# A first layernorm transposed on VectorE, a router on four column parts of the array, and scatters that keep their place

## The chip, the cores and the metric

The kernel runs on one core of a Trainium2 chip. A core has engines with streams of instructions of their own: TensorE (PE in the profile; PEld is its loading of weights), VectorE (DVE), ScalarE (ACT), GpSimd (POOL) and SyncE (SP, which here only issues transfers). They wait for one another by semaphores. Operands lie in SBUF, an on-chip memory of 128 partitions; TensorE writes to PSUM, which the other engines read. Transfers to and from the chip's main memory (DRAM) are queued by an engine and carried out by DMA engines.

The metric is the time of one execution in microseconds (us), the median of several runs. Everything is computed in 32-bit floats.

## The reference

Four batches (B) of 512 tokens (L) with 512 features (D) go through a cross-attention without softmax, against a context of 1024 rows (S), and then through a mixture of eight experts (E), two for each token. There are 16 heads of 32 features (HD).

```python
def attention(query, kv, Wq, Wg, bg, Wkv, Wo):
    q = query @ Wq.T
    gate = sigmoid(query @ Wg.T + bg)
    k, v = split(kv @ Wkv.T, 2, axis=-1)
    q, k = feature_map(q), feature_map(k)     # where(x > 0, x + 1, exp(x)), head by head
    kv_summary = einsum("bhsd,bhse->bhde", k, v)
    z = 1.0 / (einsum("bhld,bhd->bhl", q, k.sum(axis=-2))[..., None] + EPS)
    attn = einsum("bhld,bhde->bhle", q, kv_summary) * z
    return attn * gate @ Wo.T

def experts(x, Wr, We, be):
    w, sel = top_k(einsum("bsd,de->bse", x, Wr), 2)
    w = softmax(w)
    # sum over the two chosen experts e of w_e * (x @ We[e] + be[e])

x = x + attention(layernorm(x), context, ...)
x = x + experts(layernorm(x), Wr, We, be)
```

A layernorm subtracts the mean of a token's 512 features and multiplies by the reciprocal of their standard deviation. There is one ahead of the attention (the first) and one ahead of the router and the experts (the second).

## The kernel before

A matmul on TensorE sums over partitions, so what is summed over must lie there. Tokens come from DRAM in rows (a tile is 128 tokens, one in each partition, by 512 features); for the products with wq, wg and the router the features must be in the partitions, and so a tile has to be turned.

**Keys and values** (`kv_tiles`). A batch's context has eight tiles of 128 rows, brought in turned already (cT). For each, `keys` has four matmuls to pk and `feature_map` (line 221: ex on DVE, 222: its exponential on ACT, 223: k on DVE); `values` has four to pv and a copy on ACT; `kv_add` sums k and v of the tile before into kvs, with four matmuls. One such turn holds TensorE for 7.8 us.

**First layernorm** (`layernorm_stats`, `normalized_T`). Lines 229 to 233 make mean and variance (mv) and rstd for four tiles of x. Each tile is then normalised on DVE (line 237, to xn), turned by four 128x128 transposes on TensorE through PSUM (line 94, to pt) and copied by ACT to xT (line 246). In the first batch this is done in the turns of tiles 3 to 6; for later batches in turns 4 to 7, after the attention's output of the batch before (`between` in the main loop).

**Query, gate, output.** `query` and `gate` have four groups of four matmuls each (pq, pg). `inverses` computes the denominators (pd) with four matmuls that use 32 of the array's columns each, beside one another (`tile_position`). `products` makes the rest, and `attention_out` multiplies by wo and adds to x on DVE (line 434).

**Router** (`choose`, a generator that yields between its steps). The second layernorm writes four tiles row, each of 512 features and two numbers more; they are turned as above (to x2T), and four matmuls a tile, of 128 tokens' features against eight columns of wr, give the logits pl. In batches 0 to 2 one tile's step stands in each of the turns 4 to 7 of the next batch's keys; in the last batch the steps stand among expert tiles. The top two are found on DVE by small operations (lines 499 to 513).

**Dispatch** (`dispatch`) computes on TensorE (pp, from both and acc, lines 524 to 530) the place of each token in the list of its expert, and POOL scatters the rows to stream in DRAM by eight indirect transfers (line 563). For batch b this stands inside the queries of batch b + 1.

**Experts** (`run`). A tile of 128 tokens of one expert is read from stream (xg, in four pieces of 32 partitions, and of, which holds two numbers for each token; line 704), turned on DVE by a block transpose (line 721: each 32x32 block is turned in place, and the loads and weights are laid out so that this suffices), multiplied (pe), the bias added on DVE (y, line 753), and scattered to result in DRAM by POOL (line 757). 17 tiles are run before the last dispatch's rows are there, and 18 more after; a branch behind them (`tc.If(many > SURE)`) holds tiles that this data does not need.

**The end.** `fetch` reads the two results of each token back (line 827), `add` weighs and adds them to x (line 840), `store` writes out (line 851). The list `begins` says after which expert tile each of 14 tiles of tokens is fetched; the last two are fetched after the branch by SP and ACT.

**What sets the order.** Matmuls and transposes stay in the order of the program, as do SP's loads (`load`, line 100). On POOL, `mark` puts a tiny memset ahead of a transfer, so that it keeps its place. The others are placed by a scheduler, tied at points by `issue_after`. A tile's buffer can be written again when all that used its contents are done; the pool big has one buffer for each tag (xT, aT), tag row has four, one for each tile. SP's transfers share eight semaphores in turn, so that a transfer also waits for the one eight places ahead of it.

Of the kernel before, what the change touches and what calls it, by code (L numbers as in the profile page):

```python
# [9 lines left out]
F32 = mybir.dt.float32  # L10
# [3 lines left out]
ALU = mybir.AluOpType  # L14
# [3 lines left out]
P = 128  # L18
B, L, S, D = 4, 512, 1024, 512
E, F = 8, 512  # L20
HD = 32
NC = D // P
NT = L // P
# [30 lines left out]
def xattn_moe_kernel(  # L54
# [32 lines left out]
    result = dram.tile([NOWHERE + 2 * L, F], F32, name="result")  # L87


    def matmul(**operands):  # L90
        tc.keep_in_program_order(nc.tensor.matmul(**operands))  # L91

# [6 lines left out]
    def load(dst, src):  # L99
        latest["load"] = nc.sync.dma_start(out=dst, in_=src)  # L100
        tc.keep_in_program_order(latest["load"])

    def load_ctx(b, s):
# [2 lines left out]
        load(t, cT[b, s])  # L106
        return t

    def load_x(b):
        tiles = []  # L110
        for t in range(NT):
            xt = xpool.tile([P, D], F32, tag="x", name=f"x_{b}_{t}")
            load(xt, x[b, t])
            tiles.append(xt)
        return tiles

    wkv_sb = wpool.tile([P, NC, 2 * D], F32, tag="wkv", name="wkv_sb")
    wq_sb = wpool.tile([P, NC, D], F32, tag="wq", name="wq_sb")
    wg_sb = wpool.tile([P, NC, D], F32, tag="wg", name="wg_sb")
    wo_sb = wpool.tile([P, NC, D], F32, tag="wo", name="wo_sb")  # L120
    wr_sb = wpool.tile([P, NC, E], F32, name="wr_sb")
    bg_sb = wpool.tile([P, NC], F32, name="bg_sb")


    we_sb = wpool.tile([P, E, NC, F], F32, name="we_sb")
    we_rows = we.rearrange("e (c f) i n -> e i f c n", f=HD)

# [16 lines left out]
    turned = [(g, 0, g * HD, P - g * HD) for g in range(NC)]  # L144
    turned += [(g, P - g * HD, 0, g * HD) for g in range(1, NC)]
    wg_in = big.tile([P, NC, D], F32, tag="aT", name="wg_in")
    load(wg_in, wg)
    for g, a, b, n in turned:
        nc.gpsimd.tensor_copy(
            wg_sb[:, :, g * P + b : g * P + b + n], wg_in[:, :, g * P + a : g * P + a + n]  # L150
        )
        load(bg_sb[b : b + n, g : g + 1], bg[a : a + n, g : g + 1])
    load(wq_sb, wq)
    load(wr_sb, wr)
    for g, a, b, n in turned:
        load(wo_sb[b : b + n, g, :], wo[a : a + n, g, :])


    ident = const.tile([P, P], F32, name="ident")
# [18 lines left out]
    for g in range(NC):  # L178
        r = slice(g * HD, (g + 1) * HD)
        for i in range(NC):  # L180
            o = (i + g) % NC
            nc.gpsimd.affine_select(
                out=spread[r, o, :], in_=spread[r, o, :], pattern=[[0, HD]],
                compare_op=ALU.is_equal, fill=0.0, base=-i, channel_multiplier=1,
            )

    ones = const.tile([P, P], F32, name="ones")
    nc.gpsimd.memset(ones, 1.0)
# [29 lines left out]
    def feature_map(dst, src):  # L218

        ex = work.tile([P, D], F32, tag="ex", name="ex")  # L220
        nc.vector.tensor_scalar(ex, src, 0.0, None, ALU.min)  # L221
        nc.scalar.activation(ex, ex, AF.Exp)  # L222
        nc.vector.scalar_tensor_tensor(dst, src, 0.0, ex, ALU.max, ALU.add)  # L223

    def layernorm_stats(tiles):
        mv = small.tile([P, NT, 2], F32, tag="mv", name="mv")
        for t in range(NT):
            st = small.tile([P, 6], F32, tag="st", name="st")
            nc.vector.bn_stats(st, tiles[t])
            nc.vector.bn_aggr(mv[:, t, :], st)  # L230
        rstd = small.tile([P, NT], F32, tag="rstd", name="rstd")
        nc.scalar.activation(rstd, mv[:, :, 1], AF.Sqrt, bias=eps_sb)
        nc.vector.reciprocal(rstd, rstd)
        return mv, rstd

    def normalize(dst, xt, t, mv, rstd):
        nc.vector.tensor_scalar(
            dst, xt, mv[:, t, 0:1], rstd[:, t : t + 1], ALU.subtract, ALU.mult
        )

    def transposed(dst, src):

        pt = pmm.tile([P, NC, P], F32, tag="mm", name="pt")
        for c in range(NC):
            transpose(pt[:, c, :], src[:, ts(c, P)])
        nc.scalar.copy(dst, pt)

    def normalized_T(xT, t, tiles, mv, rstd):

        xn = work.tile([P, D], F32, tag="ex", name="xn")  # L250
        normalize(xn, tiles[t], t, mv, rstd)
        transposed(xT[:, :, ts(t, P)], xn)

    def new_xT():
        return big.tile([P, NC, L], F32, tag="xT", name="xT")
# [199 lines left out]
    def mark():  # L455

        tc.keep_in_program_order(nc.gpsimd.memset(marked, 0.0))
# [12 lines left out]

    def choose(b, mv, rstd):

        pl = pmm.tile([P, NT, E], F32, tag="mm", name="pl")
        rows, xTs = [], []
        for t in range(NT):
            row = work.tile([P, ROW], F32, tag="row", name="row", bufs=NT)
            normalize(row[:, 0:D], xs[b][t], t, mv, rstd)
            nc.gpsimd.tensor_copy(row[:, D : D + 1], home[:, b * NT + t : b * NT + t + 1])
            rows.append(row)

        def logits(t):
            for c in range(NC):
                matmul(
                    out=pl[:, t, :],
                    lhsT=xTs[t][:, c, :],
                    rhs=wr_sb[:, c, :],
                    start=(c == 0),
                    stop=(c == NC - 1),
                )

        for t in range(NT):
            xTs.append(work.tile([P, NC, P], F32, tag="z", name="x2T"))
            transposed(xTs[t], rows[t])
            if t > 0:
                logits(t - 1)
            yield
        logits(NT - 1)
        lg = small.tile([P, NT, E], F32, tag="lg", name="lg")
        nc.vector.tensor_copy(lg, pl)

        def largest(name):
            m = small.tile([P, NT, 1], F32, tag=f"m{name}", name=f"m{name}")
            hot = small.tile([P, NT, E], F32, tag=f"hot{name}", name=f"hot{name}")
            at = small.tile([P, NT, 1], F32, tag=f"at{name}", name=f"at{name}")
            nc.vector.tensor_reduce(m, lg, AX.X, ALU.max)
            nc.vector.tensor_tensor(hot, lg, m.to_broadcast([P, NT, E]), ALU.is_equal)
            nc.vector.tensor_tensor(hot, hot, rank, ALU.mult)
            nc.vector.tensor_reduce(at, hot, AX.X, ALU.max)
            nc.vector.tensor_tensor(hot, hot, at.to_broadcast([P, NT, E]), ALU.is_equal)
            return m, hot, at  # L510

        m1, hot1, first = largest("1")
        nc.vector.scalar_tensor_tensor(lg, hot1, -BIG, lg, ALU.mult, ALU.add)
        m2, hot2, _ = largest("2")

        routed[b] = rows, m1, hot1, first, m2, hot2
        yield
# [292 lines left out]
    def fetch(t, tiles, queue, group=None):  # L810

        pool, tag = homes[t // 2 % len(homes)]
        if t not in fetched:
            pair = pool.tile([P, 2, 2, F], F32, tag=tag, name=f"y_{t}")
            fetched[t], fetched[t + 1] = pair[:, 0], pair[:, 1]
        if group is None:
            src = flat[:, t]
        else:
            if group not in rows_of:
                rows_of[group] = nc.values_load(  # L820
                    spots[0:1, group : group + 1], [queue.engine], min_val=0, max_val=NOWHERE,
                    skip_runtime_bounds_check_because="one of two constants",
                )
            row = rows_of[group] + (t - READ[group][0]) * 2 * P
            src = result[ds(row, 2 * P), :].rearrange("(p i) f -> p i f", i=2)
        mark()
        load = queue.dma_start(out=fetched[t], in_=src)
        behind(load, written["result"][:tiles], "results of the tokens")
        for put in written["result"][tiles:]:
            tc.declare_no_dep(load.ins, put.ins, reason=read_again)  # L830
        tc.keep_in_program_order(load)
        read_back.append(load)
# [31 lines left out]
    def plan(step, *what):  # L864
        at_step.setdefault(min(step, SURE), []).append(what)

    begins = (-3, -2, -1, 0, 5, 6, 7, 8, 10, 11, 14, 15, SURE - 1, SURE - 1)
    for g, (lo, hi, most) in enumerate(READ):
        for t in range(lo, hi):
            plan(begins[t], fetch, t, most, nc.gpsimd, g)  # L870
# [9 lines left out]

    xT = new_xT()
    kv_tiles(0, 0, 3)
    ln = layernorm_stats(xs[0])
    kv_tiles(0, 3, NS, lambda i: i < NT and normalized_T(xT, i, xs[0], *ln))
    kv_blocks(sums[0])
    for b in range(B):
        more = b + 1 < B
# [42 lines left out]
        next(product)  # L930
        if more:
            xs[b + 1] = load_x(b + 1)
            kv_tiles(b + 1, 0, NS // 2, inside=lambda: next(product))
        else:
            next(early)
            next(product)
            for _ in range(3):
                next(early)
        attention_out(b, aT)
        choice = choose(b, *layernorm_stats(xs[b]))  # L940
        if more:
            ln = layernorm_stats(xs[b + 1])
            xT = new_xT()

            def between(i):
                normalized_T(xT, i, xs[b + 1], *ln)
                next(choice)

            kv_tiles(b + 1, NS // 2, NS, between)
            next(choice)  # L950
            kv_blocks(sums[b + 1])
    for _ in range(2):
# [3 lines left out]
        if t % 2:  # L956
            next(early)
    next(choice)
    for _ in range(2):
        next(early)  # L960
    dispatch(B - 1)
    for _ in range(2):
        next(early)
# [113 lines left out]
```

## Time and profile before

| | |
|---|---|
| median of 3 runs | 621.65 us (619.83 to 622.51) |
| profiled execution | 622.61 us, span 621.0 us |
| mean granted TensorE clock | 0.983 |
| PE busy | 588.5 us, 95% of the span, 1908 instructions |
| DVE busy | 271.0 us, 44%, 668 instructions |
| ACT busy | 115.2 us, 19%, 180 instructions |
| POOL busy | 100.6 us, 16%, 274 instructions |
| DMA | 105.55 MB, mean 170 GB/s |

The span runs from the first instruction to the last. The slices divide it into 40 equal stretches, and each digit is the busy share of one in tenths. In a group of instructions by line, the columns are line, engine, operation, output<-inputs with shapes and how often; busy time and the mean duration in ns; and the engine's idle time just ahead of them with what ended it. A line of the timeline has a start in us, a duration in us (of the first to the last of the group that follow one another), engine, line and operation. A line of the chain has a start, the time that this step adds to the chain, the engine or DMA and what it did; a q behind an engine's name is its sequencer, which also issues transfers.

### The profile page before, as it was taken

What the parts mean: (1) busy time and instruction counts of PE and PEld (TensorE: products, weight loads), DVE (VectorE), ACT (ScalarE), POOL (GpSimd) and SP (SyncE); (2) the same over time, 40 slices, a digit from 0 to 9 for tenths busy, and PEclk for the clock granted to TensorE, in tenths of its full rate; (3) what the DMA queues carried; (4) which work ended last, traced back from release to release, by engine and by line L of the source; (5) the groups of instructions that cost most, each with busy time, mean ns of one, the idle gap of its engine ahead of it and who ended that gap; (6) DMA issues with size and microseconds to landing.
All of it is one profiled execution on the core that took longest, in us unless ns stands there. A gap on an engine that the chain in (4) does not pass through costs nothing. (4 is left out here: it accounts for less than half of the span.)

```text
span 621.0 us, 6578 instructions
## 1 busy us (share of the span) xinstructions
PE 588.5 (95%) x1908; PEld 286.3 (46%) x1908; DVE 271.0 (44%) x668; ACT 115.2 (19%) x180; POOL 100.6 (16%) x274
## 2 busy tenths in 40 slices
PE   7999999999999999999999999999999999999940
PEld 3555543454565335446643454565434554443410
DVE  2222243216215341351454226127874569475663
ACT  1322222112322221142222211322210100000000
POOL 4100000000002200000050000002311227455540
PEclk9999999999999999999999999999999999999985
DMA  8648920682686227527530660933344444889965
GB/s 317 191 158 301 293 81 2 167 240 69 164 248 184 81 86 237 153 85 221 186 137 1 203 204 0 327 130 137 116 114 119 96 119 177 262 243 259 296 219 173
DMA packets 68597, 105.55 MB, mean 170 GB/s; under 512 B 11981, under 2 KB 30413, under 8 KB 68176
## 3 DMA queue, kind: packets, MB, share of 16 engines
q1 hardware_dynamic: 58944, 76.24, 41.7%
q0 software_dynamic: 8176, 26.78, 12.1%
q10 hardware_dynamic: 1440, 2.10, 1.1%
q8 instruction: 16, 0.26, 0.2%
q14 instruction: 21, 0.17, 0.1%
HBM read 45.93 MB, written 59.94 MB: 170 GB/s over the span
## 5 line engine op out<-in xcount | busy, mean ns | idle before, releaser
L91 PE MATMUL pk<-wkv_sb,cT 128*128 128x512 f32 x256 | 118.6, 607 | 4.4 <-DMA cT<-in_cT_dram 4.4
L91 PE MATMUL pv<-wkv_sb,cT 128*128 128x512 f32 x256 | 115.2, 593 | 0.0
L221 DVE TENSOR_SCALAR ex<-pk 128x512 f32<-128x512 f32 x32 | 22.0, 688 | 148.3 <-PE pk L91 148.3
L91 PEld LDWEIGHTS pv<-wkv_sb,cT 128*128 128x128 f32 x256 | 48.4, 190 | 62.3 <-issue 59.3
L91 PEld LDWEIGHTS pk<-wkv_sb,cT 128*128 128x128 f32 x256 | 47.7, 194 | 57.8 <-issue 49.9
L91 PE MATMUL pe<-we_sb,xgT 128*128 x144 | 62.8, 595 | 0.6 <-DVE xgT L721 0.6
L91 PE MATMUL pe<-we_sb,turned_rows 128*128 x136 | 60.3, 597 | 0.7 <-DVE turned_rows L721 0.7
L278 POOL MEMSET v<- 128x4 f32 x32 | 3.3, 105 | 345.3 <-PE kvs L91 282.3
L91 PE MATMUL pg<-xT,wg_sb 128*128 128x512 f32 x128 | 56.7, 596 | 0.0
L91 PE MATMUL pq<-xT,wq_sb 128*128 128x512 f32 x128 | 56.6, 596 | 0.0
L91 PE MATMUL po<-wo_sb,aT 128*128 128x512 f32 x128 | 55.6, 592 | 0.0
L222 ACT ACTIVATE ex<-ex 128x512 f32<-128x512 f32 x48 | 30.2, 630 | 136.2 <-DVE ex L221 126.6
L757 POOL DMA_INDIRECT result<-y,to x35 | 35.8, 1023 | 93.7 <-DVE y L753 88.4
L91 PEld LDWEIGHTS pe<-we_sb,xgT 128*128 128x128 f32 x144 | 27.0, 190 | 36.3 <-issue 29.9
L91 PEld LDWEIGHTS pe<-we_sb,turned_rows 128*128 128x128 f32 x136 | 25.3, 190 | 32.4 <-issue 29.5
L563 POOL DMA_INDIRECT stream<-row,slot x32 | 31.9, 996 | 50.3 <-DVE cmp L591 22.5
L91 PEld LDWEIGHTS kvs<-v,k 128*128 128x128 f32 x256 | 33.3, 191 | 13.4 <-issue 13.4
L91 PEld LDWEIGHTS pg<-xT,wg_sb 128*128 128x128 f32 x128 | 24.0, 190 | 32.1 <-issue 32.1
L91 PEld LDWEIGHTS po<-wo_sb,aT 128*128 128x128 f32 x128 | 24.1, 190 | 29.2 <-issue 28.7
L91 PEld LDWEIGHTS pq<-xT,wq_sb 128*128 128x128 f32 x128 | 23.8, 190 | 27.3 <-issue 27.3
L91 PE MATMUL kvs<-v,k 128*128 128x129 f32 x256 | 34.0, 275 | 0.0
L223 DVE SCALAR_TENSOR_TENSOR k<-pk,ex 128x512 f32<-128x512 f32 x32 | 22.1, 690 | 19.5 <-ACT ex L222 19.5
(175 smaller groups left out, 465.1 us busy)
## 6 DMA issues: line engine op xcount, KB each, us to landing
stream<-empty SPq DMA_DIRECT2D x24, 1028.0 KB, 8.1
stream<-empty SPq DMA_DIRECT2D x8, 1285.0 KB, 6.8
xg<-stream SPq DMA_DIRECT2D x140, 64.0 KB, 2.7
we_sb<-in_we_dram SPq DMA_DIRECT2D x32, 256.0 KB, 5.5
cT<-in_cT_dram SPq DMA_DIRECT2D x31, 256.0 KB, 3.1
y<-result POOLq DMA_DIRECT2D x14, 512.0 KB, 5.5
x<-in_x_dram SPq DMA_DIRECT2D x16, 256.0 KB, 6.6
out_dram<-y POOLq DMA_DIRECT2D x10, 256.0 KB, 4.6
```

Source lines behind the costliest of these rows:

```text
L91: tc.keep_in_program_order(nc.tensor.matmul(**operands))
L221: nc.vector.tensor_scalar(ex, src, 0.0, None, ALU.min)
L222: nc.scalar.activation(ex, ex, AF.Exp)
L223: nc.vector.scalar_tensor_tensor(dst, src, 0.0, ex, ALU.max, ALU.add)
L278: nc.gpsimd.memset(v[:, :, P : P + 1], 1.0)
L563: put = nc.gpsimd.indirect_dma_start(out=stream, out_offset=bass.IndirectOffsetOnAxis(ap=slots[i][:, t, :], axis=0), in_=rows[t], in_offse ...
L757: put = nc.gpsimd.indirect_dma_start(out=result, out_offset=bass.IndirectOffsetOnAxis(ap=home_i, axis=0), in_=y, in_offset=None, bounds_ch ...
```

## The change

**First layernorm.** x is brought in a second time, as blocks (`load_blocks`): partition 32 i + t holds chunk i (128 features) of the tokens t, 32 + t and so on, in runs of 512 bytes. For blocks, mean and rstd must lie otherwise than `layernorm_stats` leaves them: `spread_moments` writes them from POOL to moments in DRAM and reads them back into ln. `normalized_T` then has four operations of 128x128 on DVE for a tile, and one block transpose of 128x512 straight to xT. In xT the features have another order within the partitions; wq and wg are loaded in the same order (`load_rows`). Both are placed in turns 0 to 3 of the next batch's keys, ahead of the attention's output, no longer in turns 4 to 7. The first batch's stay in turns 3 to 6.

**Router.** All four tiles of row are turned first, to one x2T of 512 tokens. Four matmuls, one for each chunk of 128 features, against wr padded with zeros to 32 columns, stand on four column parts and write four shares of the logits to ps. ACT copies ps to share, and four matmuls with the constant by_expert add the shares and turn the result: pl. `choose` yields once more. The four tiles of row are one tile now, whose buffer the blocks also use (tag row, one buffer).

**Order.** wo is loaded after the first three turns, not before. `fetch` has a mark ahead of its values_load, and the last pair of fetches in `begins` stands one expert tile earlier. In the last batch, one expert tile instead of two stands between the router's last matmuls and dispatch, one more between ps and pl.

```diff
+    moments = dram.tile([B, HD, NT, P // HD, 2], F32, name="moments")
...
+    def load_blocks(b):
+        blocks = work.tile([P, NT, ROW], F32, tag="row", name="blocks", bufs=1)
+        blocks = blocks.rearrange("p t r -> p (t r)")[:, 0 : NT * D]
+        for i in range(NC):
+            load(
+                blocks[ts(i, HD), :].rearrange("t (n f) -> t n f", f=P),
+                x[b, :, :, ts(i, P)].rearrange("k (j t) f -> t (k j) f", t=HD),
+            )
+        return blocks
...
+    def load_rows(dst, w):
+        for i in range(NC):
+            load(dst[ts(i, HD)], w.rearrange("(c f) i n -> i f c n", f=HD)[i])
...
-    wr_sb = wpool.tile([P, NC, E], F32, name="wr_sb")
+    wr_sb = wpool.tile([P, NC, HD], F32, name="wr_sb")
+    nc.gpsimd.memset(wr_sb, 0.0)
...
-    load(wg_in, wg)
+    load_rows(wg_in, wg)
...
-    load(wq_sb, wq)
-    load(wr_sb, wr)
-    for g, a, b, n in turned:
-        load(wo_sb[b : b + n, g, :], wo[a : a + n, g, :])
+    load_rows(wq_sb, wq)
+    blocks = load_blocks(0)
+    load(wr_sb[:, :, 0:E], wr)
...
+    by_expert = const.tile([P, E], F32, name="by_expert")
+    nc.gpsimd.memset(by_expert, 1.0)
+    for c in range(NC):
+        nc.gpsimd.affine_select(
+            out=by_expert[ts(c, HD), :], in_=by_expert[ts(c, HD), :], pattern=[[1, E]],
+            compare_op=ALU.is_equal, fill=0.0, base=0, channel_multiplier=-1,
+        )
...
-        nc.vector.scalar_tensor_tensor(dst, src, 0.0, ex, ALU.max, ALU.add)
+        latest["map"] = nc.vector.scalar_tensor_tensor(dst, src, 0.0, ex, ALU.max, ALU.add)
...
-    def normalized_T(xT, t, tiles, mv, rstd):
-
-        xn = work.tile([P, D], F32, tag="ex", name="xn")
-        normalize(xn, tiles[t], t, mv, rstd)
-        transposed(xT[:, :, ts(t, P)], xn)
+    def spread_moments(b, tiles):
+
+        mv, rstd = layernorm_stats(tiles)
+        for k, of in enumerate((mv[:, :, 0], rstd)):
+            nc.gpsimd.dma_start(
+                out=moments[b, :, :, :, k].rearrange("t n j -> j t n"), in_=of
+            )
+        ln = small.tile([P, NT, P // HD, 2], F32, tag="ln", name="ln", bufs=1)
+        for i in range(NC):
+            nc.gpsimd.dma_start(
+                out=ln[ts(i, HD)].rearrange("t n j k -> t (n j k)"),
+                in_=moments[b].rearrange("t n j k -> t (n j k)"),
+            )
+        return ln
+
+    def normalized_T(xT, t, blocks, ln):
+
+        rows = blocks[:, ts(t, D)].rearrange("p (j f) -> p j f", f=P)
+        with tc.issue_after(latest["map"].ins):
+            for j in range(P // HD):
+                nc.vector.tensor_scalar(
+                    rows[:, j], rows[:, j], ln[:, t, j, 0:1], ln[:, t, j, 1:2],
+                    ALU.subtract, ALU.mult,
+                )
+            nc.vector.transpose(
+                xT[:, :, ts(t, P)].rearrange("p c (j t) -> p j c t", t=HD),
+                rows.rearrange("p j (c f) -> p j c f", f=HD),
+            )
...
+        batch = work.tile([P, NT, ROW], F32, tag="row", name="rows", bufs=1)
...
-        def logits(t):
-            for c in range(NC):
-                matmul(
-                    out=pl[:, t, :],
-                    lhsT=xTs[t][:, c, :],
-                    rhs=wr_sb[:, c, :],
-                    start=(c == 0),
-                    stop=(c == NC - 1),
-                )
...
-            xTs.append(work.tile([P, NC, P], F32, tag="z", name="x2T"))
-            transposed(xTs[t], rows[t])
-            if t > 0:
-                logits(t - 1)
+            transposed(xT[:, :, ts(t, P)], rows[t])
             yield
-        logits(NT - 1)
+
+        ps = pmm.tile([P, L], F32, tag="mm", name="ps")
+        for c in range(NC):
+            matmul(
+                out=ps[ts(c, HD), :],
+                lhsT=wr_sb[:, c, :],
+                rhs=xT[:, c, :],
+                start=True,
+                stop=True,
+                tile_position=(0, c * HD),
+            )
+        share = work.tile([P, L], F32, tag="z", name="share")
+        nc.scalar.copy(share, ps)
+        yield
+        pl = pmm.tile([P, NT, E], F32, tag="mm", name="pl")
+        for t in range(NT):
+            matmul(
+                out=pl[:, t, :], lhsT=share[:, ts(t, P)], rhs=by_expert, start=True, stop=True
+            )
...
             if group not in rows_of:
+                mark()
...
-    begins = (-3, -2, -1, 0, 5, 6, 7, 8, 10, 11, 14, 15, SURE - 1, SURE - 1)
+    begins = (-3, -2, -1, 0, 5, 6, 7, 8, 10, 11, 14, 15, SURE - 2, SURE - 2)
...
     kv_tiles(0, 0, 3)
-    ln = layernorm_stats(xs[0])
-    kv_tiles(0, 3, NS, lambda i: i < NT and normalized_T(xT, i, xs[0], *ln))
+    for g, a, b, n in turned:
+        load(wo_sb[b : b + n, g, :], wo[a : a + n, g, :])
+    ln = spread_moments(0, xs[0])
+    kv_tiles(0, 3, NS, lambda i: i < NT and normalized_T(xT, i, blocks, ln))
...
-            kv_tiles(b + 1, 0, NS // 2, inside=lambda: next(product))
+            blocks = load_blocks(b + 1)
+            xT = new_xT()
+
+            def between(i):
+                if i == 0:
+                    ln.append(spread_moments(b + 1, xs[b + 1]))
+                else:
+                    for t in {1: (0,), 2: (1,), 3: (2, 3)}[i]:
+                        normalized_T(xT, t, blocks, ln[0])
+
+            ln = []
+            kv_tiles(b + 1, 0, NS // 2, between, inside=lambda: next(product))
...
-            ln = layernorm_stats(xs[b + 1])
-            xT = new_xT()
-
-            def between(i):
-                normalized_T(xT, i, xs[b + 1], *ln)
-                next(choice)
-
-            kv_tiles(b + 1, NS // 2, NS, between)
+            kv_tiles(b + 1, NS // 2, NS, lambda i: next(choice))
+            next(choice)
             next(choice)
             kv_blocks(sums[b + 1])
...
     next(choice)
-    for _ in range(2):
-        next(early)
+    next(early)
+    next(choice)
+    next(early)
     dispatch(B - 1)
```

More of the change, by code (lines that the diff above doesn't have):

```diff
@@ L471, in choose @@
     def choose(b, mv, rstd):
-        pl = pmm.tile([P, NT, E], F32, tag="mm", name="pl")
-        rows, xTs = [], []
+        rows = []
+        batch = work.tile([P, NT, ROW], F32, tag="row", name="rows", bufs=1)
         for t in range(NT):
-            row = work.tile([P, ROW], F32, tag="row", name="row", bufs=NT)
+            row = batch[:, t, :]
             normalize(row[:, 0:D], xs[b][t], t, mv, rstd)
@@ L479, in choose @@
             rows.append(row)
-        def logits(t):
-            for c in range(NC):
-                matmul(
-                    out=pl[:, t, :],
-                    lhsT=xTs[t][:, c, :],
-                    rhs=wr_sb[:, c, :],
-                    start=(c == 0),
-                    stop=(c == NC - 1),
-                )
+        xT = big.tile([P, NC, L], F32, tag="aT", name="x2T")
         for t in range(NT):
-            xTs.append(work.tile([P, NC, P], F32, tag="z", name="x2T"))
-            transposed(xTs[t], rows[t])
-            if t > 0:
-                logits(t - 1)
+            transposed(xT[:, :, ts(t, P)], rows[t])
             yield
-        logits(NT - 1)
+        ps = pmm.tile([P, L], F32, tag="mm", name="ps")
[16 more added lines that the diff above has]
+            )
         lg = small.tile([P, NT, E], F32, tag="lg", name="lg")
```

## The prediction

> **What bounds the kernel now.** I read the page's busy times first, then its slices, the groups of instructions by line with shapes kept apart, TensorE's timeline at the places that the change touches, and last the chain that ended last, from 590 us on.
>
> ```profile
> PE 588.5 (95%) x1908; PEld 286.3 (46%) x1908; DVE 271.0 (44%) x668; ACT 115.2 (19%) x180; POOL 100.6 (16%) x274
> PE   7999999999999999999999999999999999999940
> ```
>
> TensorE (PE) is busy in every slice but the first and the last two, so an instruction taken off its stream moves all that follows, and one put on VectorE (DVE, 44%) costs only where TensorE waits for it. These groups price the parts:
>
> ```profile
> L91 PE MATMUL pl<-wr_sb,x2T 128*128 128x8 f32 x128 | 15.4, 247 | 0.2 <-ACT x2T L246 0.2
> L721 DVE STREAM_TRANSPOSE xgT<-xg 128x512 f32<-128x512 f32 x18 | 12.7, 707 | 20.0 <-DMA xg<-stream 20.0
> L94 PE MATMUL pt<-ident,xn 128*128 128x128 f32 x64 | 9.8, 275 | 2.8 <-DVE xn L237 2.8
> L246 ACT COPY xT<-pt 128x512 f32<-128x512 f32 x16 | 9.4, 586 | 12.1 <-PE pt L94 12.1
> L237 DVE TENSOR_SCALAR xn<-x,mv,rstd 128x512 f32<-128x512 f32 x16 | 8.6, 539 | 0.1
> L591 DVE TENSOR_TENSOR cmp<-counts,steps 128x128 f32<-128x128 f32 x4 | 1.2, 293 | 0.1
> of<-stream SPq DMA_DIRECT2D x35, 1.0 KB, 2.4
> ```
>
> Matmuls overlap, so their durations overstate what they hold of the engine; starts in the timeline give the pitch. Around tile 4 of batch 1's keys, then round a product on four column parts:
>
> ```profile
> 154.00 1.06 PE L91 MATMUL kvs<-v,k 128*128 128x129 f32 x8
> 156.00 0.66 PE L94 MATMUL pt<-ident,xn 128*128 128x128 f32 x4 [0.94 <-DVE xn L237]
> 156.50 0.60 PE L94 MATMUL pt<-ident,row 128*128 128x128 f32 x4
> 156.93 3.60 PE L91 MATMUL pk<-wkv_sb,cT 128*128 128x512 f32 x8
> ...
> 165.57 0.96 PE L91 MATMUL pl<-wr_sb,x2T 128*128 128x8 f32 x8
> 166.38 3.68 PE L91 MATMUL pk<-wkv_sb,cT 128*128 128x512 f32 x8
> ...
> 205.24 1.06 PE L91 MATMUL pd<-qT,h_ks 128*32 128x512 f32 x8
> 206.23 1.98 PE L91 MATMUL pg<-xT,wg_sb 128*128 128x512 f32 x4
> ```
>
> The end, in the chain:
>
> ```profile
> 592.02 11.38 DMA out_dram<-y
> 603.41 0.09 POOLq L1012
> ...
> 604.72 2.33 DMA result<-y,to
> ...
> 607.30 6.38 DMA y<-result
> ```
>
> The last scatter starts only at 604.72, though its row was added on DVE by 597.35 + 0.69 = 598.04: it stands behind the branch of line 1012 on GpSimd (POOL), and the chain leads that back to a store begun at 592.02.
>
> **The change part by part.** All against the profiled execution's 622.61 us (span 621.0 and 1.61 around it; the median of the runs is 621.65).
>
> 1. First layernorm off TensorE. Four transposes hold the engine for 0.44 us (165.13 − 164.69 between the neighbours in the second such place, 156.93 − 156.50 here for the same form). 16 tiles: −7.0.
>
> 2. The wait ahead of them. kvs begins at 154.00 and holds 0.89 (its pitch everywhere), so the transposes were due at 154.89 and began at 156.00: 1.11, in three batches. What comes next is the transposition of row; its last input ends on DVE at 154.1, after stats of the next x that are moved away. −3.3; bounds 0 (row is as late) and −3.3.
>
> 3. Router, batches 0 to 2. Four pl groups of 0.81 (166.38 − 165.57) leave: 3.25. In come ps, which has pd's form (0.99 = 206.23 − 205.24), and four pl matmuls, whose 16 columns' worth I take as one group of 0.81, together 1.80. ps must be copied by ScalarE (ACT) before pl: nothing stands between, so TensorE waits some 0.2 for the hand-over, 0.59 for a 128x512 copy and 0.05. 3.25 − 2.66 = 0.6 a batch: −1.8. Bounds: −4.4 (the copy hidden) and 0 (ACT has h_kv copies ahead of it).
>
> 4. Router, last batch: an expert tile stands between ps and pl, so 3.25 − 1.80 and the waits of 0.41 ahead of its pl groups go: −1.85. But only one expert (3.5 us) instead of two now lies between pl and pp. lg to acc took 501.79 to 505.47 on DVE, so pp is due about 0.95 later than TensorE gets there: net −0.9, bounds −1.85 and 0.
>
> 5. Stats of the next x. They move ahead to where DVE does the top-2 of the batch before, in batches 1 and 2: four bn_stats of 0.64 pitch and four aggregations fall between lg (187.40) and acc (done 191.72). That makes it 8.7 us after pl instead of 5.3; TensorE comes to pp 7.78 after it (194.17 − 186.41): +0.6 with some hand-over, twice, +1.2. Bounds 0 (the scheduler's order lets acc go first) and +3.4 (all of the stats' time).
>
> 6. What DVE and ACT take on. Each tile has four 128x128 normalisations, of 0.2 to 0.293 each (small operations, and the cmp row), and a block transpose of 0.707, in place of 0.539: up to +1.3 us of DVE, 21 in all, spread where DVE is idle half the time; ACT loses 16 copies of 0.586. Zero, as k of a key tile is made 8 us or more ahead of its kvs. Without that cover it would be 1.3 a tile.
> [...]
>
> 7. SP's queue. x comes a second time (blocks, 1 MB a batch in runs of 512 B). In batches 1 and 2 the blocks take the buffer that the eight scatters read, so on SP they, and the cT, weight and empty-row transfers behind them, wait for those. Scatters were issued until 206.24 and land 3.2 later; blocks go at 211 to 214, cT of tile 2 lands by 220, and its pk starts at 234.76: hidden, with 13 us to spare; were that gone, each us would cost a us. At the start cT_3 (issued at 22.31) gets four blocks and eight weight pieces ahead of it, and wo's seven pieces (4.3 us of SP) behind it; it is due at 29.53, and I make it land at 28.6. 0; bounds 0 and +3 (four 256 KB pieces at 2.7 us, as xg's 64 KB in such runs, in place of what wo took).
>
> 8. Moments. Mean and rstd go to DRAM in 512 pieces of 4 bytes each and come back, all on POOL's queue. The nearest row is of: 128 pieces of 8 bytes in 2.4 us, so at most 9.6 a write, some 22 for both and the reading. In the first batch rstd is there at 20.2; normalisation comes after k_3's map (35.2), and DVE in order holds ex of k_4 behind it, which TensorE doesn't miss before kvs at 52.79, so before 48.3 on DVE. 28 us of room: 0. Batch 1 and 2's later sends stand behind the scatters (206) and have until about 245.
>
> 9. The tail. The last scatter moves ahead of the branch, right behind two fetches that end at 601.26: it starts at 601.3 to 601.7, −3.0 (bounds −3.4 and 0). mark, the zeroed router columns and one more step of the router cost POOL 0.1 us each, off the path.
>
> Sum: −7.0 − 3.3 − 1.8 − 0.9 + 1.2 − 3.0 = −14.8: 607.8, so 608.
>
> **The rivals.**
>
> A: the gains of items 3, 4 and 9 come back as waits: share behind h_kv (0), pp late by 1.7 in two batches, cT_3 late by 3, the end still set by a DMA, as the chain's 11.38 us of out_dram before the branch may show when two fetches and a scatter share the engines. For it: ACT and DVE are in order there. Against it: the scatter's own input is long ready. Then 622.6 − 7.0 − 3.3 + 3.4 + 3 = 618.7 with all of it, 612 to 618 with parts.
>
> B: the moves are made but hidden anyway: TensorE's transposes leave, and what it feeds (DVE's chain k, row, acc) sets the pace, so about 620 to 622. Against it: no slice of TensorE has slack.
>
> C, slower: the moments come late. 512 pieces of 4 bytes are unlike any row. If a write behaves as four of the slow transfers of the start (stream<-empty, 257 KB, 13.5 us) in a row, it takes 54 us, the loop 56: 28 past the room, so 622.6 − 14.8 + 28 = 636. It decides from 43 us on (28 of room and 14.8 of gain). Against it: the row of small pieces, 2.4 us. [...]
>
> **How the numbers follow.** 0.62 for the forecast (603 to 611.5), 0.20 for A, 0.05 for B, 0.13 for C. About 0.5%, 3.1 us, is what a measurement tells here. Faster 0.82, same 0.05, slower 0.13. The low end is the sum with the better bounds, 622.6 − 7.0 − 3.3 − 4.4 − 1.85 − 3.4 = 602.7, taken as 603; the high end takes in A up to 618 and leaves out B and C.
>
> **What would show it.** pt<-ident,xn gone and no wait on DVE before the rows' transposes; ps followed by a gap near 0.85 to ACT; pp preceded by a gap near 0.6; the last scatter at about 587 to 588 with TensorE's end 12 us earlier; k_4's ex soon after its pk. Wrong if ln is what DVE waits for longest, if pk waits for cT_3, or if the scatter still follows a store.

## The result, and the profile after

The changed kernel takes 623.05 us (median of 20 runs, 620.09 to 629.03), the kernel before 621.11 (20 runs, 619.41 to 624.33). The ratio is 1.0041, 95% interval 1.0027 to 1.0055: slightly slower, where 608 was predicted. Its profiled execution took 622.51 us, span 620.9; that of before, 622.61, was 1.5 us above its own median, which is why the two spans look alike.

The page of the changed kernel, busy times, slices of TensorE and of its clock, and the group of pk:

```profile
PE 578.9 (93%) x1780; PEld 271.3 (44%) x1780; DVE 290.7 (47%) x732; ACT 109.6 (18%) x168; POOL 124.5 (20%) x309
PE   7959999999999999999999999999999999999940
PEclk9969999999999999999999999999999999999985
L94 PE MATMUL pk<-wkv_sb,cT 128*128 128x512 f32 x256 | 121.3, 619 | 13.0 <-DMA cT<-in_cT_dram 13.0
```

TensorE has 9.6 us less to do, as meant. But the third slice, which was full, is half empty and its clock is at 0.6, and pk, whose only idle time before was the 4.4 us at the very start, waits 13.0 us for cT. TensorE's timeline round that place, the kernel before first, then the changed one:

```profile
28.64 1.05 PE L91 MATMUL kvs<-v,k 128*128 128x129 f32 x8
29.53 3.60 PE L91 MATMUL pk<-wkv_sb,cT 128*128 128x512 f32 x8
32.96 3.60 PE L91 MATMUL pv<-wkv_sb,cT 128*128 128x512 f32 x8
```

```profile
28.80 1.06 PE L94 MATMUL kvs<-v,k 128*128 128x129 f32 x8
38.61 6.53 PE L94 MATMUL pk<-wkv_sb,cT 128*128 128x512 f32 x8 [8.75 <-DMA cT<-in_cT_dram]
44.97 3.60 PE L94 MATMUL pv<-wkv_sb,cT 128*128 128x512 f32 x8
```

pk of tile 3 waits 8.75 us, and then its eight matmuls take 6.53 in place of 3.60: pv starts 12.0 us later than before (44.97 against 32.96). Everything else can be read by following such starts through the two traces:

| TensorE's start of | before | after | after − before |
|---|---|---|---|
| pv, batch 0, tile 3 | 32.96 | 44.97 | +12.01 |
| pq, batch 0 | 71.09 | 81.38 | +10.29 |
| po, batch 0 | 133.40 | 143.68 | +10.28 |
| pq, batch 1 | 187.22 | 193.88 | +6.66 |
| po, batch 1 | 250.28 | 257.29 | +7.01 |
| pq, batch 2 | 304.10 | 307.49 | +3.39 |
| po, batch 2 | 367.16 | 370.90 | +3.74 |
| pq, batch 3 | 420.98 | 421.10 | +0.12 |
| po, batch 3 | 467.85 | 468.01 | +0.16 |
| pe behind the last pp | 508.77 | 507.67 | −1.10 |
| first late pe | 533.91 | 533.54 | −0.37 |
| end of the last pe | 597.31 | 596.66 | −0.65 |
| the last fetch (SP) | 607.30 | 606.96 | −0.34 |

So the change does win what was forecast of it on TensorE, 3.62 us in each of three batches, and gives it all away in the first 45 us. The router's place in batch 0 to 1, in the changed kernel's timeline:

```profile
190.21 1.06 PE L94 MATMUL kvs<-v,k 128*128 128x129 f32 x8
191.19 1.07 PE L94 MATMUL ps<-x2T,wr_sb 128*32 128x512 f32 x8
192.97 1.06 PE L94 MATMUL pl<-by_expert,share 128*128 128x8 f32 x8 [0.70 <-ACT share L547]
193.88 7.11 PE L94 MATMUL pq<-xT,wq_sb 128*128 128x512 f32 x16
...
201.53 0.39 PE L94 MATMUL pp<-acc,ones 128*128 128x8 f32 x2 [0.17 <-DVE acc L584]
```

From ps to pq it takes 2.69 us (193.88 − 191.19), the gap behind ACT's copy included. pp waits for acc, as foreseen, but briefly.

Why cT_3 came late: SP's timeline in the changed kernel.

```profile
9.24 2.84 SPq L103 DMA_DIRECT2D wg_in<-in_wg_dram  x4
12.40 6.75 SPq L103 DMA_DIRECT2D bg_sb<-in_bg_dram  x7
19.89 1.99 SPq L103 DMA_DIRECT2D wq_sb<-in_wq_dram  x4
21.93 3.71 SPq L103 DMA_DIRECT2D blocks<-in_x_dram  x4
25.76 5.77 SPq L103 DMA_DIRECT2D wr_sb<-in_wr_dram  x1
31.63 2.22 SPq L103 DMA_DIRECT2D cT<-in_cT_dram  x2
```

SP comes to cT_3 at 31.63 (22.31 before), and it lands some 7 us later. The step that stands out is the issue of wr, a transfer of 16 KB: that one instruction held SP for 5.77 us (0.43 before). The padded wr is brought in shorter pieces, but that is not the reason: in the kernel with its first batch left to TensorE (below), which brings it in the same pieces, the same issue takes 0.61 us. By this time the DMA engines are full. Their use in two stretches (columns: stretch in us, length, busy time and count of PE, PEld, DVE, ACT, POOL, then clock, DMA share, GB/s), before and after:

```profile
15.00:30.00 15.00, 15.00 (x49) 7.59 (x48) 4.87 (x12) 5.82 (x8) 2.88 (x9) 1.00 0.69 198
30.00:46.00 16.00, 16.00 (x57) 8.59 (x56) 3.68 (x6) 3.02 (x5) 0.21 (x2) 1.00 0.50 166
```

```profile
15.00:30.00 15.00, 14.86 (x47) 7.47 (x45) 5.04 (x13) 5.88 (x8) 3.34 (x3) 1.00 0.99 133
30.00:46.00 16.00, 7.39 (x11) 3.27 (x12) 0.69 (x1) 0.10 (x1) 4.71 (x12) 0.68 0.87 169
```

From 15 to 30 us the engines are busy 0.99 of the time and move 133 GB/s, where before they moved 198 at 0.69. And the transfers in flight between 15 and 46 us, of the changed kernel (the last column is us to landing):

```profile
DMA packets 5515, 4.70 MB, mean 152 GB/s; under 512 B 1718, under 2 KB 3766, under 8 KB 5514
...
blocks<-in_x_dram SPq DMA_DIRECT2D x4, 256.0 KB, 12.7
...
moments<-mv POOLq DMA_DIRECT2D x1, 2.0 KB, 11.7
moments<-rstd POOLq DMA_DIRECT2D x1, 2.0 KB, 12.7
```

Before, the same stretch had 3236 packets for 5.62 MB. Wr and the moments are small transfers and land late here (12.0 us for wr's 16 KB, 4.7 before; 11.7 and 12.7 for the moments' 2 KB). The blocks, of 256 KB each, are not small; what the trace shows of them is short runs: 2048 packets of 512 B to 2 KB (3766 − 1718) where before had none, in all 1.7 times the packets, less data, and full engines.

At the end, the chain of the changed kernel:

```profile
601.83 4.87 DMA result<-y,to
...
606.96 6.40 DMA y<-result
```

The last scatter does start 2.9 us earlier than before (601.83 against 604.72), and takes 4.87 us of the chain where it took 2.33. All but 0.3 us of the gain is gone before the next step.

### The profile page after: what moved, and what is told of

Its sections match the earlier page's. It is cut to its first block, busy times and chain, and to the rows that moved or that the text cites. A ratio compares the mean times of both kernels' runs of the same rounds, so it can differ in the third digit from the quotient of the medians.

```text
span 620.9 us, 6442 instructions
## 1 busy us (share of the span) xinstructions
PE 578.9 (93%) x1780; PEld 271.3 (44%) x1780; DVE 290.7 (47%) x732; ACT 109.6 (18%) x168; POOL 124.5 (20%) x309
## 4 chain that ended last, share of the span: by engine, by line
PE 72%; DMA 9%; DVE 7%; SPq 4%; issue 4%; POOL 2%; DVEq 0%; ACT 0%; POOLq 0%; ACTq 0%
PE pk L94 17%; PE pv L94 16%; PE pg L94 9%; PE po L94 9%; PE pq L94 7%; PE pe L94 6%; PE kvs L94 4%; DMA cT<-in_cT_dram 3%; DMA xg<-stream 2%; SPq L760 2%; SPq L103 2%; PE pn L94 1%; DMA wg_in<-in_wg_dram 1%; DMA of<-stream 1%; PE pt L97 1%
## 5 line engine op out<-in xcount | busy, mean ns | idle before, releaser
L94 PE MATMUL pk<-wkv_sb,cT 128*128 128x512 f32 x256 | 121.3, 619 | 13.0 <-DMA cT<-in_cT_dram 13.0
L619 POOL DMA_INDIRECT stream<-rows,slot x32 | 32.8, 1025 | 31.8 <-DVE cmp L647 21.9
```

The costliest lines, as they stand in the source:

```text
L619: put = nc.gpsimd.indirect_dma_start(out=stream, out_offset=bass.IndirectOffsetOnAxis(ap=slots[i][:, t, :], axis=0), in_=rows[t], in_offse ...
```

## The experiments

All times stand against the kernel before, run beside them.

**The loads of the keys first.** The obvious suspect is the order on SP's queue.

```diff
     load(bg_sb[b : b + n, g : g + 1], bg[a : a + n, g : g + 1])
-    load_rows(wq_sb, wq)
-    blocks = load_blocks(0)
-    load(wr_sb[:, :, 0:E], wr)
...
     kv_tiles(0, 0, 3)
+    load_rows(wq_sb, wq)
+    blocks = load_blocks(0)
+    load(wr_sb[:, :, 0:E], wr)
```

> The changed kernel with one thing moved: wq, the first batch's blocks and wr are loaded after the first three turns of the keys, so cT_3 and cT_4 stand ahead of them on SP's queue. Theory Q (cT_3 is late because it stands behind the 2048 runs of 512 bytes of blocks and the pieces of wq and wr on one queue): cT_3 is issued at about 20 us and lands by 28, TensorE's wait of 8.75 us ahead of pk of tile 3 and the half-clock group behind it (6.53 against 3.60 us) go, and the time is 623 - 12 = about 611 us, 1.6% under before. Rival M (the 4-byte writes of the moments, 18.8 to 33.4 us, clog the DMA engines whatever stands where): cT_3 is issued at 20 but lands after 33, and at most 5 us are won (618 or more). A new wait may show: DVE for ln ahead of the first normalisation.

614.6 us, ratio 0.9889 (0.9851 to 0.9928): the change wins 1.1% with nothing but this moved, though not all of the 12 us expected. cT_3 is issued at 20.54 and TensorE doesn't wait for it. But the wait isn't gone, it is at cT_5:

```profile
28.93 3.60 PE L94 MATMUL pk<-wkv_sb,cT 128*128 128x512 f32 x8
...
47.86 5.40 PE L94 MATMUL pk<-wkv_sb,cT 128*128 128x512 f32 x8 [3.25 <-DMA cT<-in_cT_dram]
```

and SP's timeline of this kernel shows why:

```profile
24.23 7.79 SPq L103 DMA_DIRECT2D blocks<-in_x_dram  x4
32.69 2.42 SPq L103 DMA_DIRECT2D wr_sb<-in_wr_dram  x1
35.15 8.04 SPq L103 DMA_DIRECT2D wo_sb<-in_wo_dram  x7
44.07 0.83 SPq L103 DMA_DIRECT2D cT<-in_cT_dram  x2
```

Theory Q (the order) holds for cT_3; yet the transfers behind it hold SP for as long as before, and the next cT pays 3.25 us of waiting and 1.8 of slow matmuls. The moments didn't hold up a cT that stands ahead of blocks, so rival M falls as the only cause. Their loop through DRAM was slow all the same: rstd is there at 19.65, ln's loads are issued at 33.65 and take 9 us, and the first normalisation starts at 44.49, 25 us after rstd. The blocks land late as well, 13.0 us after their issue (median), so which of the two it waited for isn't settled.

**One cause at a time taken away at the start.** Three kernels, each with one thing of the changed one undone or left out.

```diff
         ln = small.tile([P, NT, P // HD, 2], F32, tag="ln", name="ln", bufs=1)
+        if b == 0:
+            nc.gpsimd.memset(ln[:, :, :, 0], 0.0)
+            nc.gpsimd.memset(ln[:, :, :, 1], 1.0)
+            return ln
```

> The changed kernel without the first batch's trip of the moments through DRAM: ln of that batch is filled with mean 0 and reciprocal deviation 1 by two memsets, so its attention sees x not normalised; all else is as in the changed kernel. Rival M: cT_3 lands by about 30 us and the wait of 8.75 us all but goes. Theory Q: cT_3 still stands behind blocks, wq and wr; the wait is 7 us or more.

```diff
         for i in range(NC):
+            if b == 0:
+                load(blocks[:, ts(i, D)], x[b, i])
+                continue
```

> The changed kernel with the first batch's blocks brought in whole rows, 512 runs of 2 KB in place of 2048 runs of 512 bytes, the same 1 MB by the same four transfers at the same place. They then lie wrongly for the transposition, so the first batch's attention sees mixed-up features; the instructions are the same. Theory R (the number of short runs is what fills the DMA engines): SP's issue of wr takes far less than 5.77 us and TensorE's wait for cT_3 falls from 8.75 to under 5. Rival S (the megabyte itself, ahead of cT_3, is what costs): the wait stays above 7.

```diff
-    load_rows(wg_in, wg)
+    load(wg_in, wg)
...
-    load_rows(wq_sb, wq)
+    load(wq_sb, wq)
```

> The changed kernel with wg and wq loaded as before, one transfer each, in place of four with runs of 2 KB. The order of the features in their partitions then doesn't match xT's, so queries and gates are wrong in value; the instructions are the same. If the pieces of the weights hold up the queue, blocks are issued some 3 us earlier than 21.93 and the wait for cT_3 falls by 3 us or more; if the blocks and the moments alone do it, it falls by less than 1.5.

pk of tile 3 in TensorE's timeline, without the moments' trip:

```profile
34.11 6.45 PE L94 MATMUL pk<-wkv_sb,cT 128*128 128x512 f32 x8 [4.71 <-DMA cT<-in_cT_dram]
```

with whole rows in blocks:

```profile
35.70 6.23 PE L94 MATMUL pk<-wkv_sb,cT 128*128 128x512 f32 x8 [5.88 <-DMA cT<-in_cT_dram]
```

and with plain weights:

```profile
32.65 5.40 PE L94 MATMUL pk<-wkv_sb,cT 128*128 128x512 f32 x8 [3.31 <-DMA cT<-in_cT_dram]
```

Of 8.75 us of waiting, 4.0 go with the moments' trip, 2.9 with the short runs of blocks and 5.4 with the weights' pieces; the kernels took 619.41, 618.73 and 616.51 us, in one run each. None alone is the cause. What was expected of the weights is met, but 3.31 us of waiting stay. The other two fall between their theories: the trip takes away more than theory Q allowed and less than rival M asked; with whole rows the issue of wr is as short as R said, but the wait isn't under 5. Together the three would be more than the whole (12.3), so they act on one thing. SP's timelines show how: with plain weights SP comes to blocks at 17.85 in place of 21.93, and without the trip or with whole rows the issue of wr takes 3.39 and 0.61 us in place of 5.77. It is one queue that each part lengthens, at its front or by filling the engines behind it. And the queue is not all: with plain weights SP issues cT_3 at 22.79, only 0.5 us later than before, but the transfer takes 9.8 us to land (5.0 before), and that makes the wait that is left. Packets alone don't measure it either: from 15 to 46 us there are 3963 with whole rows, 5375 without the trip and 5358 with plain weights.

These are single runs, and two of them with the same start differ. The kernel that has its last scatter ahead of the fetches (below) starts as the changed one does, and its profile has

```profile
36.91 5.34 PE L94 MATMUL pk<-wkv_sb,cT 128*128 128x512 f32 x8 [7.30 <-DMA cT<-in_cT_dram]
```

So 1.5 us between such runs mean nothing. Counted from 7.30, 1.4 us would go with the short runs, and whether they matter by themselves isn't settled; 2.6 and 4.0 would go with the trip and with the weights' pieces.

**The first batch left to TensorE.** Of the three causes in the first batch, two go (blocks and moments); the weights' pieces stay.

```diff
-    blocks = load_blocks(0)
...
-    ln = spread_moments(0, xs[0])
-    kv_tiles(0, 3, NS, lambda i: i < NT and normalized_T(xT, i, blocks, ln))
+    moments_0 = layernorm_stats(xs[0])
+
+    def by_tensor(t):
+        xn = work.tile([P, D], F32, tag="ex", name="xn")
+        mv, rstd = moments_0
+        nc.vector.tensor_scalar(
+            xn.rearrange("p (c i f) -> p i c f", c=NC, i=NC),
+            xs[0][t].rearrange("p (i c f) -> p i c f", c=NC, i=NC),
+            mv[:, t, 0:1], rstd[:, t : t + 1], ALU.subtract, ALU.mult,
+        )
+        transposed(xT[:, :, ts(t, P)], xn)
+
+    kv_tiles(0, 3, NS, lambda i: i < NT and by_tensor(i))
```

> The changed kernel with the first batch's layernorm on TensorE as before (normalised on DVE with the features put in the new order, four transposes, a copy by ACT); no blocks and no moments for that batch, all else as changed. By theory (the start loses what the rest wins) the wait for cT_3 is under 1.5 us, 4 x 0.44 of transposes come back, and what the trace of the changed kernel won between the first query and the last expert, 10.9 us, shows in full: about 611 us, 1.7% under before (609.5 to 613). If what was won later is lost again once everything comes 12 us earlier (experts waiting for their rows, the end set by transfers), it is 615 or more.

612.39 us, ratio 0.9866 (0.9840 to 0.9892), as expected. The start is whole again, so the weights' pieces cost nothing by themselves, only on top of the other two; and the engines are less full, in the two stretches as above:

```profile
29.31 3.60 PE L94 MATMUL pk<-wkv_sb,cT 128*128 128x512 f32 x8
```

```profile
15.00:30.00 15.00, 15.00 (x48) 7.68 (x47) 4.65 (x12) 5.60 (x8) 2.87 (x9) 1.00 0.90 195
30.00:46.00 16.00, 16.00 (x56) 8.55 (x55) 3.67 (x6) 3.11 (x6) 0.21 (x2) 1.00 0.68 192
```

Four groups of transposes came back (0.44 us each), and still this is better than the changed kernel by 1.7%. po of batch 3 starts at 457.57, 10.3 us ahead of before. The last pe ends at 588.50, 8.8 ahead: a part is given back in the late tiles, which now wait 2.7 us in all for rows turned on DVE (0.6 before):

```profile
584.80 3.70 PE L94 MATMUL pe<-we_sb,xgT 128*128 x8 [1.80 <-DVE xgT L776]
```

**The tail alone, put on the kernel before.**

```diff
             if group not in rows_of:
+                mark()
...
-    begins = (-3, -2, -1, 0, 5, 6, 7, 8, 10, 11, 14, 15, SURE - 1, SURE - 1)
+    begins = (-3, -2, -1, 0, 5, 6, 7, 8, 10, 11, 14, 15, SURE - 2, SURE - 2)
```

> The kernel before with the change's tail alone: the last pair of fetches one expert tile earlier in the list, and a mark ahead of the row number's load. As predicted (item 9): the last scatter starts 3 us earlier and the end comes 3.0 us earlier, about 618 us. Rival D (the scatter now shares the DMA engines with the two fetches issued just ahead of it): the scatter starts 3 us earlier but takes nearly twice as long to land (4.9 against 2.3 us in the chain), and the end moves by less than 0.5 us, about 621 us.

622.83 us, ratio 1.0012 (0.9990 to 1.0034): nothing. The chain of this kernel:

```profile
601.27 5.62 DMA result<-y,to
...
607.15 6.44 DMA y<-result
```

The scatter starts at 601.27 and the last fetch at 607.15, against 604.72 and 607.30. Rival D holds: started straight behind two fetches of 512 KB, the scatter takes 5.6 us in place of 2.3. Before, the same two fetches stand ahead of it too, but it starts 3.5 us behind them. POOL issues them at 599.7 to 600.9 here, 600.3 to 601.5 in the changed kernel and 600.1 to 601.3 before, and by the chain the scatter has landed at 606.9, 606.7 and 607.1: its own start hardly moves that. That it is the sharing of the engines and not, say, the scatter's own data, is what the next edit was to test.

**The last scatter ahead of the fetches.** The mark stays, the list is put back.

```diff
-    begins = (-3, -2, -1, 0, 5, 6, 7, 8, 10, 11, 14, 15, SURE - 2, SURE - 2)
+    begins = (-3, -2, -1, 0, 5, 6, 7, 8, 10, 11, 14, 15, SURE - 1, SURE - 1)
```

> The changed kernel with the last pair of fetches where the list had it before (the mark stays): on POOL the last scatter then stands ahead of the two fetches and of the branch. Theory D: with no fetch issued just ahead of it the scatter lands in about 2.4 us; it can start at about 599.5 instead of 601.8 us, so the last two fetches start at 602 to 603 instead of 607, and the kernel gains 2 to 4 us on the changed one (619 to 621 us), unless the two fetches, now later, collide with the last two and take it back. By the prediction's item 9 (the place alone counts) it gains 2.3 us.

622.27 us, ratio 1.0007 (0.9988 to 1.0027), against the changed kernel's 1.0041 (1.0027 to 1.0055): some 2 us better by the ratios, at the low end of what was expected, with intervals that touch. In its profile the last fetch starts at 602.35, 4.6 us earlier than in the changed kernel's; but TensorE is through 2.1 us earlier in this run (594.55 against 596.66), after the shorter wait at the start shown above, so at most the rest is due to the edit. And then the fetch itself takes longer:

```profile
593.91 8.09 DMA result<-y,to
...
602.35 7.74 DMA y<-result
```

The chain here leads back to the scatter of 593.91, so its 8.09 us is not the last scatter's time, and it does not settle how long that one took. Fetches of 512 KB, scatters and stores share the engines at the end, and a part of what the start of the fetch gains its duration pays: 7.74 in place of 6.40.

> The same with the last pair of fetches where the list had it before, so that the last scatter stands ahead of them. From the profile of that edit alone (the last fetches started at 602.35, but took 7.74 us in place of 6.40) I expect 1 to 3 us under the kernel without it: 608 to 610. If the transfers at the end only trade places, it is within 0.5 us.

The same edit on the kernel with its first batch on TensorE: 610.78 us, ratio 0.9828 (0.9800 to 0.9857), the best kernel here, 1.7% under before. The 1.6 us between its median and that of the kernel without this edit point the way that was expected. The two intervals overlap; set directly against each other, the six runs of each differ by 2.4 us in the mean, with a 95% interval of 0.3 to 4.5. A gain is likely, and its size is open.

**The router alone, put on the kernel before.** Wr padded, all of `choose` and its extra step as changed; the first layernorm, loads and tail as before.

> The kernel before with the router's part of the change alone (four transposes, four column parts, one copy by ACT, four sums; the first layernorm, the loads and the tail as before). As predicted (items 3 and 4) it wins 0.6 us in each of three batches and 0.9 in the last, 2.7 in all: about 618 us, ratio 0.9957. The rows are ready no earlier here, so TensorE's wait on DVE ahead of the transposes (1.11 us, three times) stays. Rival: the wait for the copy and the later pp take it back, or experts wait for their rows later on, and the ratio is 0.998 to 1.001.

619.99 us, ratio 0.9966 (0.9942 to 0.9989), as predicted within the interval. From po of one batch to pq of the next it takes 53.11 us in its timeline (185.84 − 132.73), where before has 53.82: 0.71 a batch. In the last batch po to the first pe behind pp takes 39.66 in place of 40.92, and of those 1.26 us 0.73 go to

```profile
523.76 7.13 PE L91 MATMUL pe<-we_sb,turned_rows 128*128 x16 [1.48 <-DVE turned_rows L736]
```

a wait that was 0.75 before.

## Why the prediction was wrong

Item by item, from the table of starts and the lines above:

| item | predicted | measured |
|---|---|---|
| 1 to 3, batches 0 to 2 to the next | −3.47 each (1.76 + 1.11 + 0.6) | −3.62 each |
| 1, the first batch's own transposes | −1.76 | −1.72 (12.01 to 10.29) |
| 4, router in the last batch | −0.9 | −1.26, of which 0.73 is lost to a later wait |
| 5, pp waits | +0.6, twice | +0.35, twice |
| 6, DVE and ACT | 0 | no new wait for xT; DVE's busy time +19.7 (21 predicted) |
| 7, SP's queue at the start | 0, bounds 0 and +3 | +12.0 (+9.1 in the other run with this start) |
| 8, moments | 0 as a wait | 0 as a wait, but 4.0 of item 7's waiting |
| 9, the tail | −3.0, bounds −3.4 and 0 | 0 |

Items 7 and 9 make up 15.0 us, all of the 14.7 by which the profiled execution (622.51) missed 607.8.

**The step that failed is item 7**, "I make it land at 28.6. 0; bounds 0 and +3". It landed at 38.5. Three things were wrong in it. For the 28.6 no working is given, and the bound prices each block at the 2.7 us of an xg piece, which has 64 KB, a quarter of a block; the blocks took 12.7 us to land here, and 6.2 in two later batches (medians). The pieces of wg and wq were counted as eight transfers and their price was never set; taken away alone, they shorten the wait the most, by 5.4 us. And each part was weighed for itself: the moments of item 8 were costed alone, though they go through the same 16 engines in the same 15 us, and the profile of before has these at a DMA share of 0.69 in that stretch already.

**And a late load costs more than its lateness.** 8.75 us of waiting became 12.0. Read in stretches of 0.2 us, the trace has TensorE's granted clock at 0.50 from 34 to 44 us (the 0.68 above is the mean of a longer stretch), and the eight matmuls took 6.53 us in place of 3.60. The runs show the same after shorter waits, 6.45 after 4.71, 6.23 after 5.88, 5.40 after 3.25 and 3.31; yet the price doesn't grow evenly with the wait, for it was 5.34 after 7.30. The clock stood at 0.50 for 10.2 us in the changed kernel. Its mean from 30 to 46 us was 0.79 in the runs that waited 4.71 and 5.88 us and 0.89 in the one that waited 3.31; with nothing but 0.50 and 1.00 in that stretch this makes some 6.7, 6.7 and 3.5 us (an estimate). What shorter wait would have been free wasn't tried. The shortest here, 3.25 and 3.31 us, cost 1.8 us more (5.40 in place of 3.60), so the prediction's bound of +3, which has the wait alone, should have been nearly +5 (an estimate from these two runs).

**Item 9 failed much as rival A had it**, with the end still set by transfers. The scatter's new place on POOL did what it should, a start 2.9 us earlier; but the two fetches ahead of it were issued no earlier than before, and it landed 0.3 us earlier. The edit alone is worth nothing on the kernel before. That the shared engines slow the scatter fits the trace (from 600 to 605 us they move 303 GB/s, at a share of 0.88 before and 0.87 in the changed kernel), but no run shows it by itself.

**What was right.** The transposes, the wait ahead of them, the router and its copy, the late pp and the slack of DVE all came out within 0.4 us of their terms; of the first three only the router was also run by itself. Item 5 was close by luck in part: its own figures, 8.7 less 7.78 (7.76 by the two starts), make 0.9 and not the 0.6 that it took, and 0.35 was measured. Item 6 held: on DVE a tile took four operations of 339 ns mean (started every 0.28) and one of 710, some 1.9 us in all, where before it took 0.54 there and 0.44 of TensorE, and cost nothing, since no one waited. 339 ns is above the bound taken from the cmp row, 293. Rival C, the moments too late, didn't come about, but not by much: 25 us in the run with cT first, against the 28 of room; the writes of 512 pieces took 11.7 and 12.7 us, more than the 9.6 that were called the most; in two later batches they took 6.6.

Why the late tiles wait more for their rows once everything ahead of them is quicker (2.7 us against 0.6) was not tried.

## What to carry to other kernels

A load that is only moved back in a queue at a full start is not free (12.0 us here). Weigh together all that is new in that stretch, on every queue, against the DMA share that the profile shows there, and price each transfer from a row of its own size and run length; neither the bytes nor the packets alone told the delay here. Then add the slow clock: each wait of 3.25 to 8.75 us between the key tiles of these runs cost another 1.7 to 2.9 us. Work taken off the bounding engine paid as computed, but a part of it that is repeated per batch may be worth having only where its transfers have cover: here leaving the first batch as it was turns 0.4% slower into 1.3% faster. At the end of this kernel, which transfers set, an earlier issue of the scatter only made the scatter slower (4.87 us of the chain in place of 2.33).

## What the runs showed of the hardware

The issue of a transfer held SP's queue far longer when the engines were full than the 0.33 to 0.43 us of single transfers before (cT, wg, wq, wr): 5.77 us for a transfer of 16 KB in the stretch with a DMA share of 0.99. With the waits between them, four blocks took 7.79 us and seven transfers of wo 8.04 in the run with cT first (4.30 before for wo). A scatter of 128 rows took 4.5 to 5.6 us of the chain when it was issued 0.3 us behind two fetches of 512 KB (four profiles), and 2.3 when 3.5 us behind them. And TensorE's granted clock fell to 0.50 in the changed kernel's wait of 8.75 us for cT_3 and stayed there for 10.2 us; the eight matmuls of pk behind that wait took 6.53 us in place of 3.60.
